# Edge weights of a three-layer graph network: computed once and kept in DRAM

## The chip, the cores and the metric

The kernel runs on one core of a Trainium2 chip. The metric is device time in microseconds (us) of one execution. A core has five instruction streams that run side by side and meet at semaphores: TensorE (PE, its weight loads shown apart as PEld), VectorE (DVE), ScalarE (ACT), GpSimd (POOL) and SyncE (SP), with 16 DMA engines behind them. Each engine works through its own stream strictly in order, so a waiting instruction holds up all that stand behind it.

## The reference

```python
ew = edge_attr @ edge_w + edge_b                     # 100000 x 32 @ 32 x 256, the same in all layers
rel_masks = [(edge_type == i).astype(x.dtype) for i in range(NUM_REL)]
inv_cnt = [1.0 / jnp.maximum(jax.ops.segment_sum(m, dst, num_segments=n), 1.0) for m in rel_masks]
for l in range(N_LAYERS):                            # 3 layers
    residual = x
    msg = jax.nn.relu(x[src] * ew)
    out = jnp.zeros((n, D), dtype=x.dtype)
    for i in range(NUM_REL):                         # 3 relations
        h = jax.ops.segment_sum(msg * rel_masks[i][:, None], dst, num_segments=n)
        h = h * inv_cnt[i][:, None]
        out = out + h @ weights[l, i]
    out = out + x @ roots[l] + biases[l]
    x = residual + jax.nn.relu(out)
```

There are 6250 nodes with 256 features and 100000 edges, sorted by `dst`. The output is the layer norm of the input plus the result. All of it is float32. The edge weights `ew` don't depend on the layer.

## The kernel before

All the work around the change is in `ordered_path`, which builds three layers with `layer(l, ...)`, in an order that is written out by hand. A tile is 128 edges, a pair is two tiles. A layer has 391 pairs, taken in the order 64 to 390 and then 63 to 0. Two pairs share one set of buffers: one tile `xs` of 128 x 1024 (four tiles of gathered rows, 512 KB), one tile `ew_p` of the same shape in PSUM (two banks; there are two such tiles) and one tile `oh` of one-hot columns. There are 196 such sets in a layer.

The loop over `it` in `layer` takes one pair per step, and each piece of work for pair `it + k` has its own lead `k`:

- Lead 9: `gather` (L607) has POOL issue two indirect DMAs (L1054), each of which fetches 128 rows of 256 floats from `x` in layer one and from `x_mid`, the nodes of the layer before, in layers two and three. `xs` has 8 buffers (`ROWS`), so a gather may start when the reduction of the set eight earlier has read its rows. The first sets of layer one land in spare room of `x_root`, and the profile names them so. The next layer's first six pairs are gathered ahead of time by `gather_early`; rows that aren't there yet are added by `complete` (L649).
- Lead 9 too: `load_at` (L569) loads the edge attributes `at` of eight pairs, 256 KB, with SP, into one of three buffers.
- Lead 6: `seed_ew` (L616). ScalarE copies the bias `seed` from SBUF into `ew_p` (L621), for all but the first two sets of a layer, whose bias comes from a matmul in `make_ew` (L630).
- Lead 5: `make_ew` (L623). TensorE adds `at` times `ew_sb` to it, one matmul of 128 x 512 per pair (L634), which the trace records as two.
- Lead 3: `weigh` (L655). DVE multiplies `ew_p` with `xs` (L656) and ScalarE applies the rectifier (L657).
- Lead 2: `one_hot` (L667). DVE compares the edges' place and relation with a ramp (L669); in layer one ScalarE also makes a bfloat16 copy `oh_b` (L673), with which edges are counted.
- Lead 0: `reduce` (L675). TensorE sums messages by destination in `h_p` (L687 and, for counting or the other form, L690 and L695).

After that `take` (ScalarE, L703), `turn` (TensorE, L707) and `add` (DVE, L723) bring `h_p` into a ring `acc` in SBUF. Beside them `root_turn`, `root_turned`, `root_mul` and `root_keep` (L728 to L739) compute x times the root weights for one block of 128 nodes at a time; `node_mul` (L754) multiplies `acc` with the layer's weights, `node_end` (L785) forms the new nodes, SP stores them to `x_mid` (L791) in layers one and two, and `clear` (L771) zeroes a part of the ring with ScalarE. In layer three `load_x0` (L815), `deviate` and `norm` do the final norm, and SP stores the output (L808).

Within a step the program text runs in the order gather, load, reduce, take, make_ew, turn, weigh, seed_ew, root and node work, one_hot, add; each engine's stream has its share of that in that order.

## Time and profile before

| what | value |
|---|---|
| median of three runs | 2960.99 us (2960.32 to 2961.77) |
| the profiled execution's own time | 2962.1 us |
| its span, first to last instruction | 2959.9 us |
| mean granted TensorE clock in it | 0.972 of full speed |
| busy: PE, DVE, ACT, POOL | 2585.9, 1999.4, 1503.9, 2227.8 us |
| matmuls of `make_ew`, all layers (L634) | 688.5 us in 2346 |
| seed copies (L621) | 588.8 us in 582, 1012 ns each |
| moved by DMA | 387.39 MB, 131 GB/s over the span |
| of it by the gathers' queue | 307.65 MB |

A busy time of an engine counts its computing instructions, not issue, waits or the time in which a DMA is under way. A group of instructions is shown as line, engine, operation, output and inputs with their shapes and count, then its busy time and the mean ns of one, then the idle time just ahead of them and what ended most of it. A timeline row has the start, the duration, the engine and line, the operation, and in brackets the idle time ahead of it with what ended it ("issue": nothing that the profile shows). A window row has the stretch, its length, busy time and count for PE, PE's weight loads, DVE, ACT and POOL, then the granted clock, the share of the 16 DMA engines, and GB/s.

### The profile page before, as it was taken

What the parts mean: (1) busy time and instruction counts of PE and PEld (TensorE: products, weight loads), DVE (VectorE), ACT (ScalarE), POOL (GpSimd) and SP (SyncE); (2) the same over time, 40 slices, a digit from 0 to 9 for tenths busy, and PEclk for the clock granted to TensorE, in tenths of its full rate; (3) what the DMA queues carried; (4) which work ended last, traced back from release to release, by engine and by line L of the source; (5) the groups of instructions that cost most, each with busy time, mean ns of one, the idle gap of its engine ahead of it and who ended that gap; (6) DMA issues with size and microseconds to landing.
All of it is one profiled execution on the core that took longest, in us unless ns stands there. A gap on an engine that the chain in (4) does not pass through costs nothing. (4 is left out here: it accounts for less than half of the span.)

```text
span 2959.9 us, 43407 instructions
## 1 busy us (share of the span) xinstructions
PE 2585.9 (87%) x13712; PEld 1779.5 (60%) x13712; DVE 1999.4 (68%) x4910; ACT 1503.9 (51%) x1911; POOL 2227.8 (75%) x2355
## 2 busy tenths in 40 slices
PE   5999999999998778888889998778888988999876
PEld 2566677677765545556666666455555666666644
DVE  6666677778775555566767776545566777888864
ACT  4666666566565444454444444434444444444443
POOL 7777777777777777777777777777777777777776
PEclk9999999999999999999999999989999999999998
DMA  5444444444444444444444444444444444444443
GB/s 168 146 146 136 148 124 124 129 131 129 129 133 130 132 116 120 129 122 123 127 125 130 131 131 129 135 132 125 125 133 134 135 132 132 138 136 139 129 127 96
DMA packets 173705, 387.39 MB, mean 131 GB/s; under 512 B 43594, under 2 KB 79068, under 8 KB 173468
## 3 DMA queue, kind: packets, MB, share of 16 engines
q0 software_dynamic: 112608, 307.65, 36.4%
q1 hardware_dynamic: 53280, 68.50, 7.2%
q10 hardware_dynamic: 7580, 8.37, 1.0%
q8 instruction: 113, 1.85, 0.3%
q14 instruction: 124, 1.02, 0.1%
HBM read 364.89 MB, written 19.46 MB: 130 GB/s over the span
## 5 line engine op out<-in xcount | busy, mean ns | idle before, releaser
L1054 POOL DMA_INDIRECT xs<-x_mid,src_r x1540 | 1460.3, 948 | 469.1 <-issue 360.0
L657 ACT ACTIVATE xs<-xs 128x1024 f32<-128x1024 f32 (+1 forms) x585 | 615.7, 1052 | 1290.2 <-DVE xs L656 1269.8
L656 DVE TENSOR_TENSOR xs<-ew_p,xs 128x1024 f32<-128x1024 f32 (+1 forms) x585 | 711.8, 1217 | 662.0 <-DMA xs<-x_mid,src_r 433.4
L1054 POOL DMA_INDIRECT xs<-in_x_dram,src_io x770 | 731.2, 950 | 235.4 <-issue 196.8
L695 PEld LDWEIGHTS h_p<-oh,xs 128*128 128x128 f32 x5160 | 665.1, 195 | 253.7 <-issue 122.5
L695 PE MATMUL h_p<-oh,xs 128*128 128x120 f32 x5160 | 728.9, 286 | 88.7 <-issue 38.2
L634 PE MATMUL ew_p<-ew_sb,at 64*128 64x512 f32 x2346 | 688.5, 663 | 106.0 <-ACT ew_p L621 101.1
L669 DVE TENSOR_SCALAR oh<-iota_w,seg_o 128x120 f32<-128x120 f32 x2346 | 623.5, 328 | 0.0
L687 PE MATMUL h_p<-xs,oh 128*120 128x256 f32 x2088 | 571.7, 408 | 21.4 <-issue 7.4
L621 ACT ACTIVATE ew_p<-seed 128x1024 f32<-128x1024 f32 x582 | 588.8, 1012 | 0.0
L754 PE MATMUL o_p<-w_sb,acc 128*128 128x256 f32 (+1 forms) x1728 | 440.1, 391 | 30.5 <-DVE x_root L785 27.4
L687 PEld LDWEIGHTS h_p<-xs,oh 128*120 128x120 f32 x2088 | 363.7, 192 | 163.1 <-issue 50.0
L723 DVE TENSOR_TENSOR acc<-h_p,acc 128x240 f32 (+1 forms) x732 | 324.6, 443 | 184.8 <-PE o_p L754 67.9
L754 PEld LDWEIGHTS o_p<-w_sb,acc 128*128 128x128 f32 (+1 forms) x1728 | 309.4, 191 | 152.2 <-DVE x_root L785 67.3
L634 PEld LDWEIGHTS ew_p<-ew_sb,at 64*128 64x128 f32 x2346 | 182.0, 189 | 234.7 <-ACT ew_p L621 131.0
L785 DVE SCALAR_TENSOR_TENSOR x_root<-o_p,inv,x_root 128x256 f32<-128x256 f32 (+1 forms) x432 | 207.3, 480 | 27.6 <-PE o_p L754 20.9
L736 PE MATMUL r_p<-r_sb,t_s 128*128 128x256 f32 x588 | 160.8, 397 | 25.3 <-ACT t_s L732 25.0
L771 ACT ACTIVATE acc<-zero_o 128x768 f32<-128x768 f32 (+1 forms) x150 | 140.2, 935 | 15.2 <-PE o_p L754 14.6
L673 ACT ACTIVATE oh_b<-oh 128x480 bf16<-128x480 f32 x196 | 116.4, 594 | 59.0 <-DVE oh L669 58.1
L736 PEld LDWEIGHTS r_p<-r_sb,t_s 128*128 128x128 f32 x588 | 104.6, 195 | 46.2 <-ACT t_s L732 34.5
L728 PEld LDWEIGHTS r_p<-ident_o,x_all 128*128 128x128 f32 x294 | 30.6, 143 | 160.9 <-DVE x_root L739 107.1
L728 PE MATMUL r_p<-ident_o,x_all 128*128 128x128 f32 x294 | 65.1, 304 | 62.9 <-DVE x_root L739 62.1
(110 smaller groups left out, 939.3 us busy)
## 6 DMA issues: line engine op xcount, KB each, us to landing
at<-in_attr_laid_dram SPq DMA_DIRECT2D x147, 256.0 KB
xs<-x_mid,src_r POOLq DMA_INDIRECT x1540
xs<-in_x_dram,src_io POOLq DMA_INDIRECT x770
x_mid<-x_all SPq DMA_DIRECT2D x96, 128.0 KB
x_all<-in_x_dram ACTq DMA_DIRECT2D x8, 768.0 KB
x<-in_x_dram SPq DMA_DIRECT2D x48, 128.0 KB
out_dram<-x_all SPq DMA_DIRECT2D x48, 128.0 KB
w_sb<-in_L_gnn_weights_dram SPq DMA_DIRECT2D x3, 768.0 KB
```

Source lines behind the costliest of these rows:

```text
L621: nc.scalar.activation(ew_ps[q][:, :n], seed[:, None, :, :].to_broadcast([P, n, 2, D]), AF.Copy)
L634: nc.tensor.matmul(ew_ps[q][:, k].rearrange("p i d -> p (i d)"), at[half, :], ew_sb[half].rearrange("p i d -> p (i d)"), start=False, stop ...
L656: nc.vector.tensor_mul(there, ew_ps[q][:, pairs.start:pairs.stop], there)
L657: nc.scalar.activation(there, there, AF.Relu)
L669: nc.vector.tensor_scalar(ohs[q][:, i, :], iota_w[:, :, :WIN], seg[:, 4 * q + i:4 * q + i + 1], None, op0=ALU.is_equal)
L687: nc.tensor.matmul(h_p[:WK, :D], ohs[u // 2][:, t, :], xs[u // 2][:, u % 2, i, :], start=(i == 0 and first), stop=(i == 1 and closes(u)), ...
L695: nc.tensor.matmul(h_p[:, d * WK:(d + 1) * WK], xs[u // 2][:, u % 2, i, d * P:(d + 1) * P] if d < DC else full_ones, (ohs if d < DC else o ...
L723: nc.vector.tensor_tensor(there, h_ps[span][:, :CH * WK].rearrange("p (c r w) -> p c r w", c=CH, r=R), there, op=ALU.add)
L736: nc.tensor.matmul(rs[c][:, 1, :], t_ss[c][:, d, :], r_sb[:, d, :], start=(d == 0), stop=(d == DC - 1))
L754: nc.tensor.matmul(o_p[:n, j, :], acc[:, d, r, slot:slot + n], w_sb[:, r * DC + d, :], start=(d == 0), stop=(d == DC - 1))
L785: nc.vector.scalar_tensor_tensor(root, o_p[:n, j, :], inv[:n, c, r:r + 1], root, op0=ALU.mult, op1=ALU.add)
L1054: nc.gpsimd.indirect_dma_start(out=xs[:, u % 2, i, :], out_offset=None, in_=x_rows[:, :], in_offset=bass.IndirectOffsetOnAxis(ap=src_i[:, ...
```

## The change

In layer one a new step `keep_ew`, with lead 4, has ScalarE copy each finished `ew_p` from PSUM to a tile `ew_s` in SBUF, and SP store it to a DRAM tile `ew_all` of its own (512 KB for each set of two pairs). `make_ew` is then built in layer one alone, and so are the loads of `at`. In layers two and three `load_ew`, with lead 10, has SP load the stored tile into `ew_s` (three buffers), and `seed_ew` has ScalarE copy it into `ew_p` where it copied the bias; that is all that `ew_p` needs, and the multiply of `weigh` follows. `at` has two buffers in place of three, and the loads of `at` for the next layer are gone. In the changed kernel all lines from L616 on stand lower: `seed_ew`'s copies are L633 (loaded tile) and L636 (bias), `keep_ew`'s are L625 and L626, the load is L620, `make_ew`'s matmul is L649, the multiply L671, the rectifier L672, the gather L1072.

```diff
+    ew_all = [dram.tile([P, 4 * D], F32, name=f"ew_all{q}") for q in range(-(-U // 2))]
...
     def load_at(g):
-        at = edge.tile([P, GROUP // 2, P], F32, name="at", bufs=3)
+        at = edge.tile([P, GROUP // 2, P], F32, name="at", bufs=2)
...
+        def load_ew(q):
+            n = len(pairs_of(q))
+            ew_ss[q] = edge.tile([P, 2, 2, D], F32, name="ew_s", bufs=3)
+            nc.sync.dma_start(ew_ss[q][:, :n].rearrange("p k i d -> p (k i d)"), ew_all[q][:, :n * 2 * D])
+
+        def keep_ew(q):
+            n = len(pairs_of(q))
+            ew_s = edge.tile([P, 2, 2, D], F32, name="ew_s", bufs=3)
+            nc.scalar.activation(ew_s[:, :n], ew_ps[q][:, :n], AF.Copy)
+            nc.sync.dma_start(ew_all[q][:, :n * 2 * D], ew_s[:, :n].rearrange("p k i d -> p (k i d)"))
+
         def seed_ew(q):
 
             n = len(pairs_of(q))
             ew_ps[q] = ew_pool.tile([P, 2, 2, D], F32, name="ew_p")
+            if l > 0:
+                nc.scalar.activation(ew_ps[q][:, :n], ew_ss[q][:, :n], AF.Copy)
+                return
             if len(ew_ps) > OCT // 2:
                 nc.scalar.activation(ew_ps[q][:, :n], seed[:, None, :, :].to_broadcast([P, n, 2, D]), AF.Copy)
...
-            if pair(AHEAD) is not None and pair(AHEAD) // GROUP not in ats:
+            if l > 0 and pair(LOAD_EW) is not None and first_of(it + LOAD_EW, 2):
+                load_ew(pair(LOAD_EW) // 2)
+            if l == 0 and pair(AHEAD) is not None and pair(AHEAD) // GROUP not in ats:
                 ats[pair(AHEAD) // GROUP] = load_at(pair(AHEAD) // GROUP)
...
-            if l < L - 1 and U - 10 <= it < U - 8:
-                ats_next[at_groups[it - U + 10]] = load_at(at_groups[it - U + 10])
 
             if pair(0) is not None:
                 reduce(pair(0))
...
-            if pair(5) is not None and first_of(it + 5, 2):
+            if l == 0 and pair(5) is not None and first_of(it + 5, 2):
                 make_ew(pair(5) // 2)
...
+            if l == 0 and pair(4) is not None and first_of(it + 4, 2):
+                keep_ew(pair(4) // 2)
             if pair(6) is not None and first_of(it + 6, 2):
                 seed_ew(pair(6) // 2)
...
+LOAD_EW = 10
```

ScalarE's stream in the first steps of layer one, before (the number behind a name tells the buffers' tiles apart):

```order
L621 ACTIVATE ew_p_475<-seed_237 128x1024
L673 ACTIVATE oh_b_484<-oh_479 128x480
L657 ACTIVATE xs_393<-xs_393 128x1024
L621 ACTIVATE ew_p_522<-seed_237 128x1024
L673 ACTIVATE oh_b_529<-oh_524 128x480
L657 ACTIVATE xs_419<-xs_419 128x1024
```

The same engine there in the changed kernel:

```order
L672 ACTIVATE xs_521<-xs_521 128x1024
L625 ACTIVATE ew_s_618<-ew_p_592 128x1024
L636 ACTIVATE ew_p_621<-seed_433 128x1024
L688 ACTIVATE oh_b_628<-oh_623 128x480
L672 ACTIVATE xs_544<-xs_544 128x1024
L625 ACTIVATE ew_s_651<-ew_p_621 128x1024
L636 ACTIVATE ew_p_654<-seed_433 128x1024
L688 ACTIVATE oh_b_661<-oh_656 128x480
```

Between the rectifier and the next seed stands a copy out of PSUM, of the tile that was seeded one round earlier. The multiply of that tile stands behind it by a semaphore; it waited for TensorE's semaphore before and waits for ScalarE's now.

TensorE's stream near the start of layer two, before, where `x2` counts equal rows that follow one another:

```order
L687 MATMUL h_p<-xs,oh 120x256 x2
L634 MATMUL ew_p<-ew_sb,at 128x512 x2
L687 MATMUL h_p<-xs,oh 120x256 x4
L634 MATMUL ew_p<-ew_sb,at 128x512 x2
L728 MATMUL r_p<-ident_o,x_all 128x128 x2
L687 MATMUL h_p<-xs,oh 120x256 x2
L707 MATMUL h_p<-ident_o,h_s 128x120 x2
L687 MATMUL h_p<-xs,oh 120x256 x2
L634 MATMUL ew_p<-ew_sb,at 128x512 x2
```

The same place in the changed kernel:

```order
L702 MATMUL h_p<-xs,oh 120x256 x8
L743 MATMUL r_p<-ident_o,x_all 128x128 x2
L702 MATMUL h_p<-xs,oh 120x256 x6
L722 MATMUL h_p<-ident_o,h_s 128x120 x2
L751 MATMUL r_p<-r_sb,t_s 128x256 x2
```

The two matmuls of `make_ew` per set are gone, and the reductions, the transposes and the root products keep their order.

SyncE's stream where layer one ends and layer two begins, before:

```order
L564 DMA r_sb_8693<-in_L0_gnn_roots_dram 128x2x256
L566 DMA b_sb_8695<-in_L0_gnn_biases_dram 128x256
L571 DMA at_8697<-in_attr_laid_dram 128x512
L571 DMA at_8717<-in_attr_laid_dram 128x512
L791 DMA x_mid0_226<-x_all_267 128x256
L571 DMA at_9003<-in_attr_laid_dram 128x512
```

There in the changed kernel:

```order
L626 DMA ew_all2_230<-ew_s_9478 128x1024
L626 DMA ew_all1_229<-ew_s_9511 128x1024
L626 DMA ew_all0_228<-ew_s_9544 128x1024
L806 DMA x_mid0_226<-x_all_463 128x256
L620 DMA ew_s_9649<-ew_all32_260 128x1024
L620 DMA ew_s_9651<-ew_all33_261 128x1024
L620 DMA ew_s_9653<-ew_all34_262 128x1024
```

The last store of layer one's nodes (L806, L791 before) stood behind the two loads of `at` for layer two; it stands now behind the last stores of edge weights and ahead of the first loads of layer two.

More of the change, by code (lines that the diff above doesn't have):

```diff
@@ L601, in layer @@
         r_next, ats_next, early_next = (None, None), {}, {}
-        seen, h_bank = [0], {}
+        seen, h_bank, ew_ss = [0], {}, {}
         def gather(u):
```

## The prediction

> I call two pairs of 128-edge tiles (512 edges, one `ew_p` of two PSUM banks) a quad: a layer has 391 pairs, 196 quads and 782 gathers.
>
> **What bounds the kernel now.** I began with the page, whose busy shares point at TensorE:
>
> ```profile
> span 2959.9 us, 43407 instructions
> PE 2585.9 (87%) x13712; PEld 1779.5 (60%) x13712; DVE 1999.4 (68%) x4910; ACT 1503.9 (51%) x1911; POOL 2227.8 (75%) x2355
> ...
> L1054 POOL DMA_INDIRECT xs<-x_mid,src_r x1540 | 1460.3, 948 | 469.1 <-issue 360.0
> ...
> L1054 POOL DMA_INDIRECT xs<-in_x_dram,src_io x770 | 731.2, 950 | 235.4 <-issue 196.8
> ```
>
> The 75% of POOL hides the bound. Idle time ahead of its gathers is 469.1 us over 1540, 0.305 us each, and 235.4 over 770, 0.306 each: a constant, not a wait. POOL's timeline (start, duration, and in brackets the idle time before) and its waits (sum, times, longest) say the same:
>
> ```profile
> 3.87 1.10 POOL L1054 DMA_INDIRECT x_root<-in_x_dram,src_f  x1 [1.48 <-DMA src_f<-in_src_laid_dram]
> ...
> 57.99 0.95 POOL L1054 DMA_INDIRECT xs<-in_x_dram,src_io  x1 [0.30 <-issue]
> 60.04 0.95 POOL L1054 DMA_INDIRECT xs<-in_x_dram,src_io  x1 [1.11 <-ACT t_s L732]
> ...
> 2944.03 0.95 POOL L1054 DMA_INDIRECT xs<-x_mid,src_r  x1 [0.30 <-issue]
> ```
> ```profile
> POOL xs L1054 <- issue: 563.2, 1849, 0.3
> ...
> POOL xs L1054 <- ACT t_s L732: 6.6, 19, 1.1
> ```
>
> From 3.87 to 2944.98 us POOL issues 2346 gathers (12 + 770 + 24 + 1540), one every (2944.03 - 3.87) / 2345 = 1.254 us, and the longest wait of the whole train is the 1.1 us at 60.04. The program is a train of gathers of 2941.1 us, 3.9 us ahead of it and 14.9 us behind it, in which the last rows are used. A quad takes 4 x 1.25 = 5.0 us, and the rest of the core has to keep up, no more. In layers two and three it does so with time to spare; DVE waits there for rows to land:
>
> ```profile
> DVE xs L656 <- DMA xs<-x_mid,src_r: 433.4, 236, 6.1
> ```
>
> **What goes.** The matmuls of `make_ew` in layers two and three:
>
> ```profile
> L634 PE MATMUL ew_p<-ew_sb,at 64*128 64x512 f32 x1564 | 461.6, 667 | 84.4 <-ACT ew_p L621 83.7
> ```
>
> That is 461.6 us of TensorE and the waits in front of it, 1.2 us of 5.0 in every quad. All of it lies under the train: I count it at nothing. If POOL were not the bound it would be up to 462 us; that is the first rival.
>
> **What comes in layers two and three.** One load of 512 KB per quad for 128 KB of `at`, and the seed copy reads the loaded tile in place of the bias, with the same shape and direction (1012 ns in its row); I count the copy the same. The load is issued four steps, 10 us, before its copy, and the copy stands three steps before the multiply. The price is traffic: 0.524 MB per 5.0 us is 105 GB/s, less 26 for `at`. In layer one the stores add 105 and nothing goes. These stretches (busy us of each engine, count in brackets; then granted clock, DMA share, GB/s) bound what that does to POOL:
>
> ```profile
> 25.00:50.00 25.00, 12.33 (x32) 4.54 (x31) 10.56 (x27) 15.19 (x12) 18.91 (x21) 1.00 0.75 234
> 570.00:770.00 200.00, 192.66 (x1230) 144.41 (x1229) 155.65 (x373) 118.43 (x146) 151.56 (x160) 1.00 0.45 129
> ...
> 985.00:1970.00 985.00, 846.59 (x4284) 577.82 (x4285) 622.37 (x1494) 455.22 (x559) 745.22 (x788) 0.97 0.43 126
> ```
>
> After the change layer one moves 129 + 105 = 234 GB/s and layer two 126 + 79 = 205. The stretch from 25 us had 234 GB/s at a share of 0.75, and POOL's busy time in it is 18.91 of 25, against 151.56 of 200 (18.95 of 25) at 129. So the train does not stretch: 0 us, at the high end the third rival. Gathers land later, perhaps by 1 us; that shifts all consumers alike and hits only the end, where no load is left (the last was issued ten pairs earlier).
>
> **What comes in layer one.** ScalarE copies every quad from PSUM to SBUF: 196 copies of 128x1024. That direction is not in the trace; the same shape takes 1012 ns into PSUM (L621) and 1056 within SBUF (L657), and I take 1.0 us. ScalarE has room on average (118.43 busy of 200 us, plus 40 copies, is 158), so the question is order. The copy waits for `make_ew` of its quad; behind it in ScalarE's row stand the seed of the next quad, the one-hot copy and the rectifier, and the multiply on DVE now waits for the copy as well. New chain per quad: matmul, copy, seed, next matmul.
>
> It matters where POOL has no reserve. A gather into a row buffer waits for the reduction of the quad eight earlier; at 60.04 it waited, for the matmuls that end at 58.60 + 0.67 = 59.27:
>
> ```profile
> 38.33 2.17 PE L634 MATMUL ew_p<-ew_sb,at 64*128 64x512 f32 x4 [4.15 <-DMA at<-in_attr_laid_dram]
> ...
> 41.39 2.08 PE L634 MATMUL ew_p<-ew_sb,at 64*128 64x512 f32 x4
> 43.82 2.08 PE L634 MATMUL ew_p<-ew_sb,at 64*128 64x512 f32 x4 [0.35 <-ACT ew_p L621]
> ...
> 52.44 1.13 PE L634 MATMUL ew_p<-ew_sb,at 64*128 64x512 f32 x4
> ...
> 55.74 1.13 PE L634 MATMUL ew_p<-ew_sb,at 64*128 64x512 f32 x4
> ...
> 58.60 0.67 PE L687 MATMUL h_p<-xs,oh 128*120 128x256 f32 x2
> ```
> ```profile
> 41.79 1.06 ACT L657 ACTIVATE x_root<-x_root 128x1024 f32<-128x1024 f32 x1 [9.06 <-DMA xs<-in_x_dram,src_io]
> 42.76 1.01 ACT L621 ACTIVATE ew_p<-seed 128x1024 f32<-128x1024 f32 x1
> 43.70 0.59 ACT L673 ACTIVATE oh_b<-oh 128x480 bf16<-128x480 f32 x1
> ```
>
> Quad 0's matmuls end at 38.33 + 2.17 = 40.5. Today the multiply, the rectifier (to 42.8; the set's rows lie in spare room of `x_root`) and the seed of quad 2 (to 43.8) follow, then its matmul at 43.82. With the copy, the multiply starts 1.0 later, the rectifier ends at 43.9, the copy of quad 1 at 44.9, the seed at 45.9, the matmul starts at 46.0: 2.2 late. After that TensorE's own period there is 55.74 - 52.44 = 3.3 us, and ScalarE's is 1.06 + 1.0 + 1.01 + 0.59 = 3.66; three quads at up to 0.36 would add 1.1, of which the first two fall into slack. I take 2.5 us for the reduction at 59.27, and with it for the gather at 60.04 and the whole train behind it. Bounds: 0 (the copies find gaps) and 5 (2.2 + 1.1, doubled where the clock is still cold, as in the 2.17 us of the first row against 1.13). Later gathers have more reserve and follow on the shifted train.
>
> One rule speaks against the copy: the Trainium skill, "PSUM — Partial Sum Buffer", section "PSUM bank collisions raise a hardware error", says that two engines may not access one bank at the same time, reads included. By it copy and multiply cannot share the time and the 2.2 above stands; read side by side they would leave 1.8 (copy of quad 1 from 43.5, matmul at 45.6). No row of this trace has two readers of one bank.
>
> The second tight place is the dense stretch of layer one, where TensorE works 192.66 of 200 us and falls back behind POOL:
>
> ```profile
> 816.71 0.66 PE L695 MATMUL h_p<-oh,xs 128*128 128x120 f32 x4
> 817.21 0.22 PE L695 MATMUL h_p<-oh_b,full_ones 128*128 128x120 bf16 x1
> ```
> ```profile
> 825.71 0.95 POOL L1054 DMA_INDIRECT xs<-in_x_dram,src_io  x1 [0.30 <-ACT xs L657]
> ```
>
> Counted from the layer's start, these are the end of quad 156's reduction (817.43) and the first gather of quad 164, which needs its buffer: 8.3 us, less the 0.77 from 59.27 to 60.04, is a reserve of 7.5. The seed is done 0.1 + 1.0 + 1.0 = 2.1 us after the matmul and needed 5.0 - 1.13 = 3.9 after it, so TensorE waits for nothing new: 0 us. The other end is the second rival.
>
> **Layer changes and the end.** The first gather that needs the new layer's rows started 6.1 us after the store of the last node block was issued, without a wait:
>
> ```profile
> 994.73 0.33 SPq L791 DMA_DIRECT2D x_mid<-x_all  x1
> ```
> ```profile
> 1000.82 0.94 POOL L1054 DMA_INDIRECT xs<-x_mid,src_r  x1 [0.30 <-issue]
> ```
>
> SyncE issues the new loads behind that store, so it is not delayed: 0 us. Behind the last gather TensorE's clock counts:
>
> ```profile
> 2900.00:2910.00 10.00, 7.16 (x50) 5.16 (x48) 4.41 (x10) 4.03 (x5) 7.57 (x8) 1.00 0.36 105
> 2910.00:2920.00 10.00, 9.13 (x40) 6.40 (x40) 4.41 (x10) 3.93 (x5) 7.57 (x8) 0.66 0.38 107
> 2920.00:2930.00 10.00, 6.21 (x40) 4.33 (x40) 4.41 (x10) 3.85 (x5) 7.58 (x8) 1.00 0.37 104
> ```
> ```profile
> 2910.24 1.13 PE L634 MATMUL ew_p<-ew_sb,at 64*128 64x512 f32 x4 [2.00 <-ACT ew_p L621]
> ...
> 2944.24 4.19 PE L695 MATMUL h_p<-oh,xs 128*128 128x120 f32 x32 [0.83 <-ACT xs L657]
> ```
>
> The clock falls to 0.66 over ten microseconds although TensorE was busy 7.16 of the ten before. Without `make_ew` it has about 4 of 10 left, so low stretches become frequent. If one covers the closing burst of 4.19 us, this grows by up to 3.3 (the first row's 2.17 against 1.13); I take 1.3, between 0 and 3.3. The Trainium skill, "TensorE: Matmul & The Clock Gate", section "Part 1: The HAM clock gate", lets the clock drop after an idle window of about 3.4 us. By that rule the end would cost nothing and the sum be 2.5; the trace disagrees, since the longest idle gap there is 2.00 us.
>
> **Sum**, for the profiled execution: 2962.1 (span 2959.9 and 2.2 around it) + 2.5 + 1.3 + 0 = 2965.9. The median of the runs, 2961.0, lies 1.1 lower: **2964.8 us**.
>
> **Rivals.** (1) TensorE is the bound, as 87% suggests: up to 461.6 us off, 2500. Against it stands the unbroken train; 0.02, with any other way to be faster. (2) Slower: the copy holds TensorE up in the dense stretch. DVE's multiply, now behind the copy, delays the additions that free `h_p`, or a clear of `acc` on ScalarE stands ahead of the copy. Reserve falls over some 35 quads, so the point of decision is 7.5 / 35 = 0.21 us per quad; at half of the copy (0.5) POOL loses 35 x 0.5 - 7.5 = 10 us, at all of it 27.5: 2975 to 2992. For it: ScalarE goes to 158 of 200 in strict order. Against it: no wait of TensorE for ScalarE beyond start-up in layer one. 0.27. (3) The traffic stretches the gathers. Bound: the stretch from 100 to 125 us below against 18.91 at 137 GB/s, 1.6% of 2941 us, or 47 us, 3010; the stretch at 234 GB/s speaks against. 0.06. (4) The loads come too late for their copies and the change saves no wait: SyncE stands on DVE at the node stores, yet 10 us of lead and the reserve of 14 us or more hide it: no time of its own beyond the forecast's, and within its chance.
>
> ```profile
> 100.00:125.00 25.00, 25.00 (x134) 16.58 (x134) 18.02 (x39) 17.28 (x24) 19.21 (x20) 1.00 0.46 137
> ```
>
> **How the numbers follow.** The forecast has 0.65; its own range is 2961 + 0 to 2961 + 8.3, 2960 to 2970. 0.2% is 5.9 us, about what a measurement of this kernel can tell from no change: of the 0.65 I put 0.10 above 2966.9, where both terms stand near their upper ends. So same 0.55; slower 0.10 + 0.27 + 0.06 = 0.43; faster 0.02. The range, 2960 to 2984, takes in rival 2 up to two thirds and leaves out its rest, rival 3 and rival 1.
>
> **What would show it.** Right: POOL's idle time ahead of a gather still 0.30 us throughout; one longer wait near 60 us; TensorE's busy time about 460 us less with the span unchanged; low clock more often after 985 us. Wrong: waits of POOL on reductions between 780 and 850 us (rival 2), gathers above 0.95 us on average (rival 3), or a gap in the train at 1000 or 1978 us.

## The result and the profile after

The changed kernel takes 2967.01 us (median of 17 runs, 2963.86 to 2969.79) against 2961.04 of the kernel before (17 runs, 2959.46 to 2962.98): a ratio of 1.0019, 95% interval 1.0011 to 1.0026, or 6 us more (3.3 to 7.7). A third of TensorE's matmul instructions for edge weights stayed, two thirds went, and the kernel is a little slower. The profiled execution took 2967.49 us, its span is 2965.7 us against 2959.9.

From the page of the changed kernel (span, busy time of the engines, then groups with busy time, mean ns of one and idle time before):

```profile
span 2965.7 us, 41035 instructions
PE 2305.5 (78%) x12140; PEld 1797.6 (61%) x12140; DVE 1997.0 (67%) x4910; ACT 1679.7 (57%) x2111; POOL 2229.2 (75%) x2355
...
L1072 POOL DMA_INDIRECT xs<-x_mid,src_r x1540 | 1461.6, 949 | 469.2 <-issue 383.6
...
L710 PE MATMUL h_p<-oh,xs 128*128 128x120 f32 x5160 | 769.3, 301 | 174.5 <-issue 81.4
...
L702 PE MATMUL h_p<-xs,oh 128*120 128x256 f32 x2088 | 622.0, 441 | 80.0 <-ACT xs L672 36.8
...
L625 ACT ACTIVATE ew_s<-ew_p 128x1024 f32<-128x1024 f32 x196 | 199.9, 1020 | 106.1 <-issue 61.2
...
HBM read 544.19 MB, written 121.96 MB: 225 GB/s over the span
```

POOL's row reads as it did: 949 ns a gather for 948, 469.2 us of idle time in 1540 for 469.1. That is why nothing was won (the last experiment tests it). TensorE's busy time fell by 280.4 us and not by 461.6: the matmuls that stayed take longer each (301 ns for 286 in L710, 441 for 408 in L702), under a granted clock that fell. The columns of the next view, by layers, are those of the prediction's stretches, with the clock third from the end:

```profile
0.00:985.00 985.00, 899.27 (x5181) 630.09 (x5182) 686.59 (x1682) 752.76 (x941) 743.06 (x790) 0.98 0.74 239
985.00:1970.00 985.00, 699.91 (x3496) 582.86 (x3495) 621.67 (x1496) 459.42 (x563) 745.28 (x787) 0.86 0.68 218
1970.00:2945.00 975.00, 696.25 (x3423) 575.74 (x3423) 680.80 (x1713) 463.83 (x601) 738.50 (x777) 0.87 0.70 224
```

In layers two and three the clock is 0.86 and 0.87 (0.97 and 0.96 before), and POOL's busy time in them is 745.28 and 738.50 us (745.22 and 738.33).

The 5.8 us of the span can be placed along POOL's train. Its timeline in the changed kernel (start, duration, and in brackets the idle time before):

```profile
4.46 1.10 POOL L1072 DMA_INDIRECT x_root<-in_x_dram,src_f  x1 [2.08 <-DMA src_f<-in_src_laid_dram]
...
60.91 0.94 POOL L1072 DMA_INDIRECT xs<-in_x_dram,src_io  x1 [0.54 <-ACT h_s L718]
...
102.67 0.94 POOL L1072 DMA_INDIRECT xs<-in_x_dram,src_io  x1 [1.68 <-ACT oh_b L688]
...
2947.01 0.95 POOL L1072 DMA_INDIRECT xs<-x_mid,src_r  x1 [0.30 <-issue]
```

- The first gather starts at 4.46 us, 0.6 later than before. It waits for its indices, which the change doesn't touch; in nine of the ten experiments with a full train below it starts at 3.8 to 4.0, and in the tenth (late keep) at 4.48, so this is chance.
- From there to the end of the last gather the train takes 2943.5 us for 2941.1. Two of its gathers wait, 0.54 us at 60.91 and 1.68 us at 102.67; before, one waited 1.11 us. Less the regular 0.30 that is 1.6 us of waiting for 0.8. The other 1.6 us lie in single gathers that last longer than 0.95 us, here and there, such as one of 1.80 us at 18.55 (late keep has the same at 18.64, no other profile does). In the table below this part differs by some microseconds from one profile to the next. It doesn't look like chance alone: the four kernels that load no edge weights have 2939.6 us on average (2938.6 to 2940.3), the eight that do 2941.5 (2939.4 to 2943.5). These are one profile of each kernel, and no run takes the 2 us apart.
- Behind the last gather there are 17.7 us for 14.9. TensorE's closing burst, of 32 matmul records in both:

```profile
2947.30 6.61 PE L710 MATMUL h_p<-oh,xs 128*128 128x120 f32 x32 [1.69 <-ACT xs L672]
```

It lasts 6.61 us where it lasted 4.19. This is the largest single item: 2.4 of the 2.8 us by which the end grew.

### The profile page after: what moved, and what is told of

It reads as the page before. It is cut to its first block, busy times and chain, and to the rows that moved or that the text cites. A ratio compares the mean times of both kernels' runs of the same rounds, so it can differ in the third digit from the quotient of the medians.

```text
span 2965.7 us, 41035 instructions
## 1 busy us (share of the span) xinstructions
PE 2305.5 (78%) x12140; PEld 1797.6 (61%) x12140; DVE 1997.0 (67%) x4910; ACT 1679.7 (57%) x2111; POOL 2229.2 (75%) x2355
## 4 chain that ended last, share of the span: by engine, by line
PE 32%; POOL 20%; DMA 18%; issue 14%; DVE 10%; ACT 5%; DVEq 0%; POOLq 0%; ACTq 0%
POOL xs L1072 20%; DMA xs<-x_mid,src_r 15%; PE h_p L710 8%; PE h_p L702 7%; PE o_p L769 7%; PE ew_p L649 5%; DVE xs L671 5%; DMA xs<-in_x_dram,src_io 2%; ACT xs L672 2%; PE r_p L751 2%; DVE oh L684 1%; DVE acc L738 1%; PE r_p L743 1%; DVE x_root L800 1%; ACT ew_p L633 1%
## 5 line engine op out<-in xcount | busy, mean ns | idle before, releaser
L1072 POOL DMA_INDIRECT xs<-x_mid,src_r x1540 | 1461.6, 949 | 469.2 <-issue 383.6
L672 ACT ACTIVATE xs<-xs 128x1024 f32<-128x1024 f32 (+1 forms) x585 | 615.0, 1051 | 1087.1 <-DVE xs L671 1084.1
L671 DVE TENSOR_TENSOR xs<-ew_p,xs 128x1024 f32<-128x1024 f32 (+1 forms) x585 | 711.9, 1217 | 693.3 <-DMA xs<-x_mid,src_r 466.2
L1072 POOL DMA_INDIRECT xs<-in_x_dram,src_io x770 | 730.6, 949 | 236.2 <-issue 194.7
L710 PE MATMUL h_p<-oh,xs 128*128 128x120 f32 x5160 | 769.3, 301 | 174.5 <-issue 81.4
L710 PEld LDWEIGHTS h_p<-oh,xs 128*128 128x128 f32 x5160 | 719.5, 211 | 264.4 <-issue 105.3
L702 PE MATMUL h_p<-xs,oh 128*120 128x256 f32 x2088 | 622.0, 441 | 80.0 <-ACT xs L672 36.8
L769 PE MATMUL o_p<-w_sb,acc 128*128 128x256 f32 (+1 forms) x1728 | 482.2, 419 | 86.4 <-DVE x_root L800 77.0
L702 PEld LDWEIGHTS h_p<-xs,oh 128*120 128x120 f32 x2088 | 409.1, 212 | 199.8 <-ACT xs L672 43.2
L769 PEld LDWEIGHTS o_p<-w_sb,acc 128*128 128x128 f32 (+1 forms) x1728 | 336.4, 207 | 176.6 <-DVE x_root L800 95.8
L633 ACT ACTIVATE ew_p<-ew_s 128x1024 f32<-128x1024 f32 x392 | 396.9, 1012 | 12.6 <-DMA ew_s<-ew_all 12.5
L625 ACT ACTIVATE ew_s<-ew_p 128x1024 f32<-128x1024 f32 x196 | 199.9, 1020 | 106.1 <-issue 61.2
L649 PE MATMUL ew_p<-ew_sb,at 64*128 64x512 f32 x782 | 228.6, 660 | 17.7 <-ACT ew_p L636 13.4
L800 DVE SCALAR_TENSOR_TENSOR x_root<-o_p,inv,x_root 128x256 f32<-128x256 f32 (+1 forms) x432 | 207.3, 480 | 22.6 <-PE o_p L769 15.6
L636 ACT ACTIVATE ew_p<-seed 128x1024 f32<-128x1024 f32 x194 | 198.4, 1023 | 0.0
L786 ACT ACTIVATE acc<-zero_o 128x768 f32<-128x768 f32 (+1 forms) x150 | 140.3, 935 | 19.0 <-PE o_p L769 19.0
```

What stands on the lines that cost most here:

```text
L633: nc.scalar.activation(ew_ps[q][:, :n], ew_ss[q][:, :n], AF.Copy)
L649: nc.tensor.matmul(ew_ps[q][:, k].rearrange("p i d -> p (i d)"), at[half, :], ew_sb[half].rearrange("p i d -> p (i d)"), start=False, stop ...
L671: nc.vector.tensor_mul(there, ew_ps[q][:, pairs.start:pairs.stop], there)
L672: nc.scalar.activation(there, there, AF.Relu)
L702: nc.tensor.matmul(h_p[:WK, :D], ohs[u // 2][:, t, :], xs[u // 2][:, u % 2, i, :], start=(i == 0 and first), stop=(i == 1 and closes(u)), ...
L710: nc.tensor.matmul(h_p[:, d * WK:(d + 1) * WK], xs[u // 2][:, u % 2, i, d * P:(d + 1) * P] if d < DC else full_ones, (ohs if d < DC else o ...
```

## The experiments

Times differ from the kernel before by 0 to 6 us, and the interval of each ratio reaches 2 to 3 us to either side. So hardly any two of the small experiments are told apart by their times alone; what tells is where in each profile gathers wait and what lies behind the last one. The table has one profiled execution of each kernel: waits of gathers beyond the regular 0.30 us, with the time at which each ended; the rest of the train (first gather's start to last one's end, less those waits); the stretch behind it; then the medians' difference from the kernel before on the same chip and the ratio's interval.

| kernel | waits, us (at) | rest of train | behind | time, us | ratio |
|---|---|---|---|---|---|
| before | 0.8 (60) | 2940.3 | 14.9 | | |
| changed | 0.2 (61), 1.4 (103) | 2941.9 | 17.7 | +6.0 | 1.0011 to 1.0026 |
| keep only | 3.0 (62), 0.1 (103), 0.4 (1002) | 2938.6 | 15.3 | +3.1 | 1.0002 to 1.0021 |
| load only | none | 2941.7 | 16.7 | +1.2 | 0.9995 to 1.0013 |
| warm end | 2.0 (62), 0.3 (1003) | 2939.4 | 14.9 | +2.4 | 1.0004 to 1.0022 |
| came early | 1.9 (62) | 2941.5 | 15.1 | +3.4 | 1.0003 to 1.0021 |
| late keep | none | 2943.5 | 16.9 | +5.5 | 1.0006 to 1.0024 |
| both ends | 0.4, 1.0, 1.9, 0.3 (782 to 833), 0.8 (1039) | 2942.0 | 15.1 | +2.6 | 0.9999 to 1.0018 |
| copy only | 1.8 (61) | 2939.7 | 16.4 | +2.3 | 0.9997 to 1.0016 |
| store only | none | 2939.9 | 15.6 | +0.2 | 0.9991 to 1.0009 |
| twice the loads | 1.9 (61), 1.4 (103), 1.7 (1820) | 2941.8 | 16.5 | +5.8 | 1.0009 to 1.0028 |
| all three edits | 0.7, 0.3 (825, 830), 1.6 (1002) | 2940.5 | 15.2 | +3.4 | 1.0003 to 1.0021 |

### The two halves

The storing half computes edge weights in all layers and stores them in layer one:

```diff
-            if l > 0:
-                nc.scalar.activation(ew_ps[q][:, :n], ew_ss[q][:, :n], AF.Copy)
-                return
...
-                load_ew(pair(LOAD_EW) // 2)
...
-            if l == 0 and pair(5) is not None and first_of(it + 5, 2):
+            if pair(5) is not None and first_of(it + 5, 2):
```

> The storing half of the change alone: layer one copies and stores the edge weights, layers two and three compute them again as before (the stored tiles are not read). My theory, that the gathers of POOL are one unbroken train, that layer one's copy costs two short waits near its start, and that the rest of the 6 us is the slow clock under the closing burst: the waits at 60 and near 102 us come back, TensorE's closing burst runs at full clock, 15 us behind the last gather; 0.5 to 2.5 us over the kernel before. Rival one, that ScalarE's copy costs all of it: about 6 us over. Rival two, that the traffic stretches the gathers: a third of the traffic is here, so about 2 us, spread over layer one and not at two places.

The loading half keeps nothing and loads rows of x of the same size:

```diff
-            nc.sync.dma_start(..., ew_all[q][:, :n * 2 * D])
+            r0 = q % 12 * 512
+            nc.sync.dma_start(..., x[r0:r0 + n * 2 * P, :].rearrange("(p k) d -> p (k d)", p=P))
...
-                keep_ew(pair(4) // 2)
```

> The loading half alone: layer one neither copies nor stores; layers two and three load tiles of the same size from the rows of the input x in place of stored edge weights and compute none (so their edge weights are other numbers). My theory: the train of gathers takes what it took before, and only the stretch behind the last gather grows, from 15 to about 17.5 us, since TensorE's clock is low there: 1.5 to 3.5 us over the kernel before. Rival one, ScalarE's copy in layer one: no difference, within 0.7 us. Rival two, traffic: about 4 us over, from gathers above 0.95 us in layers two and three.

Each half shows its own term of the forecast and not the other's. Storing brings back a wait near 60 us, now 3.33 us, and 15.3 us behind the last gather. Loading has no wait of a gather at all, and a slow closing burst. The gather of the storing half, and the burst of the loading half:

```profile
62.22 0.94 POOL L1069 DMA_INDIRECT xs<-in_x_dram,src_io  x1 [3.33 <-ACT h_s L715]
```
```profile
2945.01 5.46 PE L712 MATMUL h_p<-oh,xs 128*128 128x120 f32 x32 [2.86 <-ACT xs L674]
```

The times were 3.1 us over (expected 0.5 to 2.5) and 1.2 us over (expected 1.5 to 3.5). Both medians miss what was expected, both intervals reach into it, and that of the second holds no difference too.

### Copy or store

The storing half again, once with ScalarE's copy and no store, once with the store of a constant and no copy:

```diff
             nc.scalar.activation(ew_s[:, :n], ew_ps[q][:, :n], AF.Copy)
-            nc.sync.dma_start(ew_all[q][:, :n * 2 * D], ew_s[:, :n].rearrange("p k i d -> p (k i d)"))
```
```diff
-            ew_s = edge.tile([P, 2, 2, D], F32, name="ew_s", bufs=3)
-            nc.scalar.activation(ew_s[:, :n], ew_ps[q][:, :n], AF.Copy)
-            nc.sync.dma_start(ew_all[q][:, :n * 2 * D], ew_s[:, :n].rearrange("p k i d -> p (k i d)"))
+            for k in range(n):
+                nc.sync.dma_start(ew_all[q][:, k * 2 * D:(k + 1) * 2 * D], ew_sb.rearrange("p i d -> p (i d)"))
```

> ScalarE's copy alone: layer one copies each tile of edge weights to SBUF, nothing is stored or loaded, layers two and three compute as before. If ScalarE's order makes the wait near 60 us (my theory): it is 2 to 3.3 us here too, DVE stands about as long for the load of source numbers as before (6 us), and the time is 1 to 3 us over the kernel before. If the stores' traffic makes it: the wait is 1 us and the time that of before.

> The stores alone: layer one stores as many bytes at the same places of SyncE's stream, but from the constant weights in SBUF (two stores of 256 KB per set), ScalarE copies nothing, and layers two and three compute as before. My theory: the wait near 60 us is as before (1 us or less), DVE stands longer for the load of source numbers than before (7 to 9 us for 6.2), and the time is 0 to 1.5 us over the kernel before. If traffic is what counts: about 3 us over, as with copy and store.

The copy alone makes the wait near 60 us, the store alone has none:

```profile
61.13 0.94 POOL L1068 DMA_INDIRECT xs<-in_x_dram,src_io  x1 [2.08 <-ACT h_s L714]
```

The store does something else. Near 85 us DVE stands for the 768 KB load of source numbers (`came`), which is issued right ahead of the compare that needs it. Before, with the copy alone and with the store alone, in this order:

```profile
88.21 2.45 DVE L585 TENSOR_SCALAR came<-came,node_i 128x128 f32<-128x128 int32 x12 [6.24 <-DMA came<-in_src_dram]
```
```profile
88.67 2.44 DVE L586 TENSOR_SCALAR came<-came,node_i 128x128 f32<-128x128 int32 x12 [4.94 <-DMA came<-in_src_dram]
```
```profile
89.44 2.44 DVE L586 TENSOR_SCALAR came<-came,node_i 128x128 f32<-128x128 int32 x12 [8.02 <-DMA came<-in_src_dram]
```

6.24 us of waiting, 4.94 and 8.02. In the changed kernel it is 8.76, and the compare starts 4.0 us later than before. ScalarE issues this load in its own stream, behind the copies. The issue before, then the issue and the compare in the changed kernel:

```profile
80.97 0.35 ACTq L582 DMA_DIRECT2D came<-in_src_dram  x1
```
```profile
83.10 0.35 ACTq L583 DMA_DIRECT2D came<-in_src_dram  x1
```
```profile
92.25 2.44 DVE L586 TENSOR_SCALAR came<-came,node_i 128x128 f32<-128x128 int32 x12 [8.76 <-DMA came<-in_src_dram]
```

So the load is issued 2.1 us later, and from there to the compare it takes 9.15 us for 7.24, another 1.9. The halves show one part each: with the copy alone the issue is at 83.33 (5.34 us to the compare), with the store alone at 80.41 (9.03 us).

### The load of source numbers issued earlier

```diff
+            if l == 0 and it == 10:
+                load_came()
             if l == 0 and it == 20:
                 find_came()
```

> The changed kernel with one edit: in layer one the 768 KB load of source numbers that DVE compares (came) is issued ten steps earlier than the compare, not right ahead of it. In the changed kernel DVE stood 8.8 us for that load (6.2 before), and the gather at 102.67 us waited 1.7 us a little later. My theory: that wait goes, DVE doesn't stand there, and the time is about 1.4 us below the changed kernel: 4 to 5 us over the kernel before. If the gather's wait has another cause (ScalarE's order alone), it stays, and the time is 6 us over.

DVE no longer stands there. The reduction that the gather near 102 us needs ends at 91.95 us, where it ended at 101.90 in the changed kernel, and the gather starts without a wait:

```profile
102.62 0.95 POOL L1076 DMA_INDIRECT xs<-in_x_dram,src_io  x1 [0.30 <-ACT ew_p L638]
```

So the second wait of the changed kernel comes through the load, which the copies delay at its issue and the stores on its way. How long it is depends on how early the train arrives: of the four kernels that start alike (changed, keep only, warm end, twice the loads) it is 1.4, 0.1, 0 and 1.4 us. The time is 3.4 us over, a little below the expected 4 to 5; this profile's closing burst ran at full clock (15.1 us behind the last gather) without any edit for it.

### TensorE kept busy at the end

The last 24 sets of layer three compute their edge weights as before:

```diff
+        def made(q):
+            p = order.index(2 * q)
+            return l == 0 or p < 0 or (l == L - 1 and p >= U - 48)
...
-            if l > 0:
+            if not made(q):
                 nc.scalar.activation(ew_ps[q][:, :n], ew_ss[q][:, :n], AF.Copy)
```

> The changed kernel, but the last 24 sets of layer three (48 pairs, the last 120 us) compute their edge weights on TensorE as before, so that TensorE is as busy there as before. My theory: the closing burst runs at full clock more often, the stretch behind the last gather goes back from 17.7 to about 15 us, and the time is 2 to 3 us below the changed kernel, that is 3 to 4 us over the kernel before. If the longer end comes from elsewhere (the loads, the output's store), it stays at 6 us over.

```profile
2944.89 4.09 PE L716 MATMUL h_p<-oh,xs 128*128 128x120 f32 x32 [0.80 <-ACT xs L678]
```

4.09 us for the burst and 14.9 behind the last gather, as before the change. The three kernels with this edit (both ends and all three edits are the others) have 14.9 to 15.2 us there; the five that load to the end have 15.1, 16.5, 16.7, 16.9 and 17.7. (Of those that compute to the end anyway, keep only has 15.3 and store only 15.6; copy only has 16.4, since its last rows landed late: its last multiply waited 1.73 us for them, the one before the change 0.36.) The mean of the five is 16.6, that of all seven that compute to the end 15.4: 1.2 us on average, and 2.8 in the changed kernel's profile. The burst itself says the same: 4.12 to 6.61 us in the five, 5.5 on average, against 4.09 to 4.37, 4.2 on average, in the kernel before and the three with the edit. The time is 2.4 us over by the medians, 1.2 to 6.5 by the interval; expected were 3 to 4.

### No copies at the start: where the time went instead

The first 24 sets of a layer are neither stored nor loaded, alone and together with the warm end; the third kernel adds the early load of source numbers. The lines of the second (the first has `U - 0` in place of `U - 48`):

```diff
+            return l == 0 or p < 48 or (l == L - 1 and p >= U - 48)
...
-            if l == 0 and pair(4) is not None and first_of(it + 4, 2):
+            if l == 0 and it + 4 >= 48 and pair(4) is not None and first_of(it + 4, 2):
                 keep_ew(pair(4) // 2)
```

> The changed kernel, but the first 24 sets of a layer (48 pairs) are neither copied nor stored in layer one, and layers two and three compute them as before. My theory, now that storing alone cost 3 us and loading alone 1 us, with gathers waiting 2 to 3.3 us near 60 us in most kernels that copy: that wait goes back to about 1 us, the closing burst stays slow, and the time is 1 to 3.5 us over the kernel before, 2.5 to 5 below the changed one. Rival, that the copies cost along the whole of layer one: no better than the changed kernel.

> The edit of the late copies and that of the warm end together: 24 sets at the start of each layer and 24 at the end of layer three are computed as before, all the others are stored and loaded. My theory: both terms are gone, and although 75% of the removed matmuls of layers two and three stay removed, the time is that of the kernel before, within 1.5 us: the work in between is worth nothing in either direction. Rival, traffic along the whole run: 3 to 5 us over still.

> Both ends computed as before and the load of source numbers issued ten steps earlier. My theory: the wait near 60 us as before, none near 100 us, full clock at the end; 2 us below to 1 us over the kernel before. The train itself, 2346 gathers at 1.251 us, gives no more: faster than 2955 us would speak against it as the bound.

The wait near 60 us is gone in all three, as expected. The time is not, and all three medians miss what was expected: 5.5, 2.6 and 3.4 us over. With both ends, gathers wait in the dense stretch of layer one instead:

```profile
782.09 0.94 POOL L1078 DMA_INDIRECT xs<-in_x_dram,src_io  x1 [0.67 <-issue]
...
788.07 0.94 POOL L1078 DMA_INDIRECT xs<-in_x_dram,src_io  x1 [1.29 <-issue]
...
827.46 0.95 POOL L1078 DMA_INDIRECT xs<-in_x_dram,src_io  x1 [2.21 <-issue]
```
```profile
826.53 0.22 PE L716 MATMUL h_p<-oh_b,full_ones 128*128 128x120 bf16 x1
```

The last row is the end of the reduction of set 156 (the prediction's quad) in that kernel, at 826.75; the gather that needs its buffer is the one at 827.46. In the changed kernel the same two events stand so:

```profile
825.80 0.22 PE L710 MATMUL h_p<-oh_b,full_ones 128*128 128x120 bf16 x1
```
```profile
827.30 0.95 POOL L1072 DMA_INDIRECT xs<-in_x_dram,src_io  x1 [0.30 <-issue]
```

827.30 less 826.02 is 1.3 us, where it was 8.3 before. A gather that waits follows the reduction by about 0.7 (827.46 less 826.75), so 0.6 us of reserve is left of 7.5. Copies alone leave 3.6 us between the two events (826.65 less 823.02) and stores alone 6.6 (824.93 less 818.34). So the delay at the start and the one in the dense stretch don't add: a train that started late by 2 us is what keeps the dense stretch from making it later still. Take the first away and the second shows, in two of the three kernels; in the third, the late keep, the events stand 1.1 us apart, 0.4 above the least.

How the copy eats the reserve is seen at 771 us. The changed kernel's DVE (first fence), TensorE and ScalarE there, then granted clock and busy times in the five microseconds:

```profile
771.20 0.53 DVE L738 TENSOR_TENSOR acc<-h_p,acc 128x360 f32 x1 [1.64 <-ACT acc L786]
```
```profile
771.79 1.01 PE L710 MATMUL h_p<-oh,xs 128*128 128x120 f32 x4 [2.50 <-DVE acc L738]
```
```profile
768.15 1.03 ACT L625 ACTIVATE ew_s<-ew_p 128x1024 f32<-128x1024 f32 x1 [0.30 <-PE ew_p L649]
769.07 1.02 ACT L636 ACTIVATE ew_p<-seed 128x1024 f32<-128x1024 f32 x1
770.02 1.15 ACT L786 ACTIVATE acc<-zero_o 128x1152 f32<-128x1152 f32 x1
```
```profile
770.00:775.00 5.00, 3.21 (x14) 2.26 (x14) 2.00 (x3) 2.72 (x4) 3.78 (x5) 0.70 0.73 239
```

The clear of the ring (L786) stands behind the copy in ScalarE's stream, a microsecond of work more; DVE's addition into the cleared place waits 1.64 us for it; TensorE waits 2.50 us for the addition, since that frees `h_p`; and its clock averages 0.70 in these five microseconds. Before, TensorE's wait there was 0.62 us and the clock 1.00:

```profile
769.31 0.71 PE L695 MATMUL h_p<-oh,xs 128*128 128x120 f32 x4 [0.62 <-DVE acc L723]
```
```profile
770.00:775.00 5.00, 4.84 (x31) 3.54 (x30) 4.93 (x13) 3.45 (x5) 3.78 (x5) 1.00 0.36 106
```

This place is the largest single loss: TensorE's reductions are 5.8 us later than in the kernel before at 767 us, and 8.6 later from 780 to 830. With copies alone the two numbers are 2.8 and 5.6, with stores alone 0.9 and 0.9.

The late keep by itself misses by most (1 to 3.5 us over expected; 5.5 by the medians, 1.8 to 7.1 by the interval). Its profile has no wait anywhere, a first gather that is 0.6 us late, a slow burst, and the longest rest of a train in the table. Whether its median is chance or has a cause of its own stays open.

None of these versions beats the kernel before. With 2346 gathers at 1.251 us each, 3.9 us ahead and 14.9 behind, the least span that this train allows is some 2954 us, or 2956 of time (an estimate from these rows and the 2.2 us by which the time exceeds the span before).

### More traffic

In layers two and three each load is followed by a copy of the same tile from DRAM to DRAM:

```diff
             nc.sync.dma_start(ew_ss[q][:, :n].rearrange("p k i d -> p (k i d)"), ew_all[q][:, :n * 2 * D])
+            nc.sync.dma_start(spare[q % 4][:, :n * 2 * D], ew_all[q][:, :n * 2 * D])
```

> The changed kernel with each load of stored weights in layers two and three followed by a copy of the same 512 KB from DRAM to DRAM, so that these layers move about 325 GB/s in place of 220. My theory: gathers keep issuing every 1.25 us as long as the row buffers' reserve holds, so 0 to 3 us over the changed kernel. Rival, that traffic stretches the train: gathers above 0.95 us or waits for row buffers, and 20 us or more over.

```profile
985.00:1970.00 985.00, 705.37 (x3487) 587.57 (x3484) 618.98 (x1492) 458.33 (x561) 744.13 (x786) 0.85 0.90 322
1970.00:2945.00 975.00, 693.01 (x3412) 576.29 (x3412) 679.70 (x1713) 463.09 (x602) 738.32 (x778) 0.86 0.92 330
```

At 322 and 330 GB/s, with the DMA engines 90 and 92% busy, POOL's busy time is that of before, and the time is the changed kernel's within the interval. One gather of these layers waited, 1.98 us at 1820. The rival that traffic stretches the gathers falls at its price of up to 47 us. What may be left of it are the 2 us by which the kernels that load exceed the others in the table's rest of the train; the rest is no longer here (2941.8 us) than with the plain loads.

### The train cut in half

The question of a large edit with a small effect is where the gain went. Both kernels were built with a shorter train: POOL gathers one tile of each pair, and SyncE loads the other as 128 neighbouring rows. That leaves out half of the gathering by index, so the messages are other numbers; all other work is the same.

```diff
-                gather_pair(nc, xs[u // 2], x_rows, src_i if l == 0 else src_r, u)
+                nc.gpsimd.indirect_dma_start(
+                    out=xs[u // 2][:, u % 2, 0, :], out_offset=None, in_=x_rows[:, :],
+                    in_offset=bass.IndirectOffsetOnAxis(ap=(src_i if l == 0 else src_r)[:, 2 * u:2 * u + 1], axis=0))
+                nc.sync.dma_start(xs[u // 2][:, u % 2, 1, :], x_rows[3 * P:4 * P, :])
```

> The kernel before with a train half as long: POOL gathers one tile of each pair, and SyncE loads the other as 128 neighbouring rows of the same table (the same bytes, the wrong rows). My theory, that POOL's train is the bound and TensorE comes next: 780 fewer... that is 1155 gathers of 1.25 us less, TensorE busy over 90% of the span, 2620 to 2800 us. If something else holds the steps together (DMA traffic, DVE), the time falls less, to 2850 or more.

> The changed kernel with the same shorter train. My theory: here the removed matmuls are worth something; layer one stays near 950 us, bound by TensorE and ScalarE's order, layers two and three take 700 to 800 us each in place of about 880: 2350 to 2600 us, at least 150 us below the kernel before with the same shorter train. If the gain isn't hidden by the train but is eaten by loads or by the slower clock, the two come out within 50 us.

2613.0 us without the change (ratio to the kernel before 0.8825, 0.8809 to 0.8841) and 2398.1 with it (0.8099, 0.8084 to 0.8114). From their pages, the kernel without the change first:

```profile
PE 2488.9 (95%) x13712; PEld 1743.0 (67%) x13712; DVE 1996.9 (76%) x4910; ACT 1504.7 (58%) x1911; POOL 1130.4 (43%) x1200
...
PE 90%; DVE 4%; issue 2%; DMA 2%; ACT 1%; POOL 0%; SPq 0%; DVEq 0%; ACTq 0%
```
```profile
PE 2103.6 (88%) x12140; PEld 1655.2 (69%) x12140; DVE 1973.3 (82%) x4910; ACT 1677.2 (70%) x2111; POOL 1130.5 (47%) x1200
...
PE 52%; DMA 21%; DVE 13%; issue 7%; ACT 5%; SPq 1%; DVEq 0%; ACTq 0%; POOL 0%; POOLq 0%
```

With the train out of the way TensorE ends last (90% of the chain), and there the change takes 215 us off. The first is 7 us below the expected range, which began at 2620, the second within. So the gain of the change exists, and in the real kernel it lies under POOL's gathers.

## Why the prediction was right

The forecast was 2964.8 us, the time is 2967.0: 2.2 us above it and within the forecast's own range of 2960 to 2970. That the kernel is slower at all is clear of noise. The line that the prediction drew between no change and slower, 0.2% or 2966.9 us, runs through the measurement (median 2967.01, ratio 1.0011 to 1.0026), so that choice was not decided by the runs.

That the number came so close is in part luck. The two terms of the sum add up to 3.8 us, and at their two places the profile has 0.9 (the gather at 60.91, before at 60.04) and 2.8. The other 2.1 of its 5.8 us lie where the sum had nothing: 1.1 up to the gather at 102.67 (100.75 before) and 1.1 in the longer gathers after it.

- **The bound and the first rival.** Shown: idle time per gather unchanged, and 215 us of gain as soon as the train is halved.
- **The term of 2.5 us at the start** was the right mechanism at the right place, mis-sized. Five experiments that copy from the start have waits of 2.08 to 3.33 us near 60 us, those without copies there none; against the 1.11 before that is 1.0 to 2.2 us more. In the changed kernel's own profile it was 0.54 us. There the train reached the place 1.4 us late (0.6 from the first gather, the rest from the one of 1.80 us at 18.55), so less was left to wait, and the first attributes had come 0.6 us early. Where the gather starts tells more than how long it waits: at 60.9 to 62.2 us, 61.5 on average, in the six kernels that copy from the start, before at 60.04. That is 0.9 to 2.2 us later, 1.5 on average, for 2.5. The chain itself is as long as the step had it: from the first matmul to that of set 2 it is 45.19 - 37.73 = 7.46 us below, before it was 43.82 - 38.33 = 5.49, so 1.97 us longer where the step had 2.2.

```profile
37.73 2.17 PE L649 MATMUL ew_p<-ew_sb,at 64*128 64x512 f32 x4 [4.24 <-DMA at<-in_attr_laid_dram]
...
45.19 2.08 PE L649 MATMUL ew_p<-ew_sb,at 64*128 64x512 f32 x4 [2.32 <-ACT ew_p L636]
```

- **Missing from the sum**: the wait at 102.67, 1.4 us. The prediction counted traffic only as something that stretches gathers, and the copies only for the edge weights' own chain. It took no look at a load that ScalarE issues behind the copies and that DVE stands on.
- **The term of 1.3 us at the end** was right in its mechanism and, on average, in its size: the burst of the five kernels that load to the end is 1.3 us longer than in those that compute there. In the changed kernel's profile it was 2.8 for the whole end. That the burst falls into a slow stretch is chance from run to run, but likely: it did in four of the five. The changed kernel's 17 runs spread over 5.9 us, those before over 3.5.
- **The 0 us in the dense stretch** was right as a number and wrong in its reason. The step said that TensorE waits for nothing new there, since the seed is ready in time. TensorE waits for DVE's addition, which waits for the clear behind the copy, much as the second rival had it (there the clear stood ahead of the copy). Of the reserve of 7.5 us some 0.6 was left: that rival was half a microsecond from coming true. In the kernel with both ends its mechanism did come true, though with 3.6 us of waits and not the 10 to 27.5 us of its price.
- **0 us for traffic on the gathers** holds up to 330 GB/s but for the 2 us that no run takes apart. The traffic itself was put too low, 205 GB/s in layer two for a measured 218: `at` is 64 KB a quad, not 128, so the loads add 92 GB/s and not 79.
- **"TensorE's busy time about 460 us less"** was wrong: 280. The matmuls that stayed took longer under the slower clock, 133 us more in the three largest groups (L710, L702 and L769, the product with the layer's weights); the rest of the 180 isn't taken apart. It cost nothing, under the train.
- **The fourth rival**, late loads, cost nothing, as the prediction had it: four copies of stored tiles waited for their loads, 12.5 us in all and 5.5 at most, and no gather of layers two and three waited.
- **The layer change** was put at 0. The changed kernel has no wait there; three experiments have one gather waiting 0.6 to 1.9 us at 1002, which no run here takes apart.

## What to carry to other kernels

Read the idle time ahead of each instruction of a queue before its busy share: here 75% busy with a constant 0.3 us between instructions was a full queue, and work taken from another engine was worth nothing. A copy that is added to an in-order engine is paid for by all that stands behind it, so count its reserve at every tight place; and waits at several tight places of one train don't add: a train that is late already waits less at the next, so curing the first may only uncover the second. If a price depends on a clock, sparse work can make the last dense piece dearer.

## What the runs showed that was not expected

A gather by index costs POOL 0.95 us and 0.30 us between two, whether the DMA engines move 126 or 330 GB/s. And a clock that falls can hide much of a saving in the busy column (280 us for 461.6).

TensorE's clock fell without long rests. In layers two and three of the changed kernel some rests of its matmuls reach 6.0 us, so the mean of 0.86 alone doesn't show it; the end does. The longest idle time of the matmuls from 2925 us on is the 2.98 us of the first row here. The window rows below it are the 3.41 us before the clock's fall at 2942.92 us and the 3.41 us after it:

```profile
2942.34 3.27 PE L710 MATMUL h_p<-oh,xs 128*128 128x120 f32 x16 [2.98 <-ACT xs L672]
```
```profile
2939.51:2942.92 3.41, 0.58 (x5) 0.58 (x6) 2.21 (x5) 1.69 (x2) 2.80 (x3) 1.00 0.40 113
2942.92:2946.33 3.41, 2.69 (x14) 2.41 (x12) 1.45 (x3) 0.43 (x2) 2.50 (x4) 0.50 0.33 91
```

The trace's record of the clock has only full and half speed, and from one change to the next a multiple of 3.41 us. In the changed kernel it falls 111 times. In the 3.41 us before each fall TensorE was busy 52% of the time or less, while a rest of 3.4 us or more in the 6.8 us before it stands behind 19 of them only. Before the change there are 39 falls, the share is 51% or less, and 6 have such a rest. Stretches of the same length at full clock that no fall followed had at least 43%.

The rule that the prediction weighed (the Trainium skill, "TensorE: Matmul & The Clock Gate", section "Part 1: The HAM clock gate"), that the clock drops after an idle window of about 3.4 us, would have left the end at full speed if it takes a full window of rest. The trace agrees with the length of the window, 3.41 us, and disagrees with that reading: here the clock dropped after a window in which TensorE was busy 0.58 us, and elsewhere after windows that were half busy.
